# FFN width 2752 as 2560 rows by Strassen and 192 rows without

## The chip, the cores and the metric

The kernel runs on one core of one Trainium2 chip. The metric is the device time of one execution in microseconds; before the change it is 2451.41 us, the median of three runs (2449.39 to 2451.61). Everything is computed in f32.

The names of the engines in the profile: PE is TensorE's matmul, PEld its weight load, DVE is VectorE, ACT is ScalarE, POOL is GpSimd, SP is SyncE, which here issues most of the DMAs.

## What is computed

`x` has 32 samples of 64 positions by 1024 features, in all 2048 tokens. Four residual layers follow each other. The last one is an FFN with low-rank adapters, and it is the one that changes:

```python
x = x + L0(x)                       # a long convolution over the feature axis
x = x + einsum('bsi,boi->bso', x, w1[ids1])     # one 1024x1024 weight for each sample
x = x + einsum('bij,bkj->bik', x, w2[ids2])     # the same again
# L3, with H = 1024, F = 2752, rank 16, one adapter for each sample
gate = x @ W_gate.T + 0.5 * (x @ A_gate.T) @ B_gate.T
up   = x @ W_up.T   + 0.5 * (x @ A_up.T)   @ B_up.T
act  = silu(gate) * up
x = x + act @ W_down.T + 0.5 * (act @ A_down.T) @ B_down.T
```

`A_*` and `B_*` are chosen for each sample by an index that is read on the device.

## The kernel before

Tokens run along the free axis and features along the partitions. The 2048 tokens are four chunks `c` of 512 (8 samples); `x` of a chunk is a tile of 128 partitions x 8 x 512. The program first does the convolution for all chunks, then the two adapter layers for chunk 0 (`adapter`, matmuls at L176, one 512 KB weight `wa` after the other), then `ffn(c)` for each chunk. The adapter layers of chunk c + 1 are cut into 16 pieces that `between` and `other` place among the FFN's matmuls of chunk c, at a rate that spreads them over the chunk: a piece falls due after a share of the hidden products and of the down products. The first piece falls due in the first tile. `x` of chunks 2 and 3 is parked in HBM (`park`) and loaded again (L454) in the first tile of the chunk before, into the buffer of a chunk that has been written out.

The FFN's hidden rows are split in two halves of 1376, each into eleven tiles `m` of up to 128 rows, so that the last tile of each half has 96. A tile `m` takes the same rows from both halves, and its products are done by the Strassen-Winograd scheme with seven instead of eight products of half the size: `stationary` (L337 to L340) forms four sums of weight quarters on VectorE, `moving` (L344 to L347) four sums of the token side, `product` (L367) runs 28 matmuls of 128x128 weights with 256 tokens for `gate` and 28 for `up`, and L381 to L396 gather the seven results from PSUM. In `gated`, before this, `gather` (L214) fetches the tile's rows of `B` from HBM by an indirect DMA on POOL into the one buffer `bgu`, `expand` (L309) runs 16 matmuls of 32 rows for the low-rank part, which lie side by side in the array four at a time, and ACT copies their four banks to `lt` (L319). Then `silu` and the multiplication give `act` (L402 to L404).

The tiles go in two blocks, six and five. After a block the down projection runs over four row blocks `h`, each with seven accumulators in four PSUM banks and one set of matmuls (L507) for each of up to three tiles. The low-rank part of `W_down` is first contracted (`low_rank_down`, L266, into `tm_d`, L278 to L284); in the last block `expand_down` (L292) adds it with matmuls of 64 rows, two side by side. L531 to L542 add the result to `x`, and after the last block L546 writes it out. In the last two row blocks the next chunk's `prepare` runs the contraction with `A_gate` and `A_up` (also L266) and forms the token sums.

The order on PE is the order of the program text; the other engines' orders come from a scheduler. PSUM has eight banks, taken in turn. Weights of all kinds share nine buffers of 512 KB (`wpool`), loaded by SP in order.

The lines that set the width before the change:

```python
F = 2752
FH = F // 2
FM = (FH + P - 1) // P        # 11
BLOCKS = ((0, 6), (6, FM))
SEG = 3
```

Of the kernel before, what the change touches and what calls it, by code (L numbers as in the profile page):

```python
# [24 lines left out]
FH = F // 2  # L25
FM = (FH + P - 1) // P
BLOCKS = ((0, 6), (6, FM))
MB = 6
# [29 lines left out]
CO_BM = CO_OFF + FM  # L58
# [4 lines left out]
def kernel(  # L63
# [18 lines left out]
    bd: bass.AP,  # L82
    out: bass.AP,
# [47 lines left out]
    il = cpool.tile([P, NCK], I32, tag="il", name="il")  # L131
    nc.sync.dma_start(il, ids_lora)
    rowf = cpool.tile([P, NCK], F32, tag="rowf", name="rowf")
# [3 lines left out]
    rows = cpool.tile([P, NCK, FM], I32, tag="rows", name="rows")  # L137
    for c in range(NCK):
        nc.vector.tensor_scalar(
            rows[:, c, :],  # L140
            cst[:, CO_OFF : CO_OFF + FM],
            rowf[:, c : c + 1],
            None,
            ALU.add,
        )
# [66 lines left out]
    def gather(table, c, piece, width, tag, name, bufs):  # L212
        t = gpool.tile([P, width], F32, tag=tag, name=name, bufs=bufs)
        nc.gpsimd.indirect_dma_start(  # L214
            out=t,
            out_offset=None,
            in_=table,
            in_offset=bass.IndirectOffsetOnAxis(
                ap=rows[:, c, piece : piece + 1], axis=0
            ),  # L220
        )
        return t
# [26 lines left out]

    FIRST, SECOND = slice(0, P // 2), slice(P // 2, P)  # L250
    tms = {}
    for name, width in (("g", 2 * H), ("u", 2 * H), ("d", TH)):
        tms[name] = hpool.tile([P, width], F32, tag=f"tm_{name}", name=f"tm_{name}")
    nc.vector.memset(tms["d"], 0.0)
# [4 lines left out]
    def low_rank(at, n, x_of, name):  # L259


        ps = ps_tile(f"pl_{name}")[:, : 2 * H]
        for i in range(n):
            x_i, k = x_of(i)
            for j in range(BC // 2):
                nc.tensor.matmul(  # L266
                    ps[pair(j)],
                    at[:k, i, pair(j)],
                    x_i[:, 2 * H * j : 2 * H * (j + 1)],
                    start=(i == 0),  # L270
                    stop=(i == n - 1),
                )
        return ps

    def low_rank_down(at, n, x_of, name, more):
        ps = low_rank(at, n, x_of, name)
        v = gpool.tile([P, 2 * H], F32, tag="tv", name=f"tv_{name}", bufs=1)
        nc.vector.tensor_mul(v, ps, bmask)  # L278
        for j in range(BC // 2):
            t = tms["d"][pair(j), 2 * H * (j % 2) :][:, : 2 * H]  # L280
            if more:
                nc.vector.tensor_add(t, t, v[pair(j)])
            else:
                nc.vector.tensor_copy(t, v[pair(j)])  # L284

    def expand_down(pairs):
# [3 lines left out]
        for two in pairs:  # L290
            for rows_, (ps, b) in zip((FIRST, SECOND), two):
                nc.tensor.matmul(  # L292
                    ps,
                    b[rows_],
                    tms["d"][rows_],
                    start=False,
# [3 lines left out]

    def expand(bt, n, name):


        banks = [ps_tile(f"pe{j}_{name}") for j in range(BC // 2)]
        for g in range(2):
            for i in range(2):
                for j, ps in enumerate(banks):
                    at_ = (2 * g + i) * 2 * H
                    nc.tensor.matmul(  # L309
                        ps[:n, at_ : at_ + 2 * H],  # L310
                        bt[pair(j), g, i, :n],
                        tms["gu"[g]][pair(j)],
                        start=(g + i == 0),
                        stop=True,
                        skip_group_check=True,
                    )
        lt = gpool.tile([P, 4, TC], F32, tag="lt", name=f"lt_{name}", bufs=1)
        for j, ps in enumerate(banks):
            nc.scalar.copy(  # L319
                lt[:n, :, 2 * H * j : 2 * H * (j + 1)],  # L320
                ps[:n].rearrange("p (i t) -> p i t", i=4),
            )
        return lt.rearrange("p (g i) t -> p g i t", g=2)
# [26 lines left out]
    def gated(c, m, xb, between):  # L350

        n = min(P, FH - m * P)
        bt = gather(bgu, c, m, 4 * P, "bgu", f"bgu_{c}_{m}", 1)
        bt = bt.rearrange("p (g i f) -> p g i f", g=2, i=2)
        lt = expand(bt, n, f"{c}_{m}")
        cs = []
        for g, w in enumerate((wg, wu)):
# [7 lines left out]
            def product(ps, j, start):  # L365
                for kt in range(KH):
                    nc.tensor.matmul(  # L367
                        ps,
                        ws[j][:, kt, :n],
# [7 lines left out]
            pa, pb, pc = (ps_tile(f"pf{i}_{name}")[:n, :TH] for i in range(3))  # L377
# [3 lines left out]
            nc.scalar.copy(u[:n], pa)  # L381
            product(pb, 5, True)
            nc.scalar.copy(cq[:n, 3], pb)  # L383
            nc.vector.tensor_add(u[:n], cq[:n, 3], u[:n])
            product(pc, 6, True)
            nc.vector.tensor_add(cq[:n, 3], pc, u[:n])
            product(pb, 4, True)
            nc.vector.tensor_add(cq[:n, 3], pb, cq[:n, 3])  # L388
            product(pa, 1, False)
            nc.scalar.copy(cq[:n, 0], pa)  # L390
            product(pb, 2, False)
            nc.vector.tensor_add(cq[:n, 1], pb, u[:n])  # L392
            product(pc, 3, False)
            nc.vector.tensor_add(cq[:n, 2], pc, u[:n])
            cf = cq[:n].rearrange("p q t -> p (q t)")
            nc.vector.tensor_add(cf, cf, lt[:n, g].rearrange("p i t -> p (i t)"))  # L396
# [4 lines left out]
        a = act[:n].rearrange("p i (t n) -> p (i t) n", t=2)  # L401
        nc.scalar.activation(a, cs[0][:n], AF.Sigmoid)  # L402
        nc.vector.tensor_mul(a, a, cs[0][:n])
        nc.vector.tensor_mul(a, a, cs[1][:n])  # L404
        return act

    def prepare(c, name):
# [3 lines left out]
        ps = low_rank(at, KT, lambda i: (x_c[:, i, :], P), f"{name}_{c}")  # L411
# [15 lines left out]
    def ffn(c, xb, others):  # L427
# [29 lines left out]

        for block, (m0, m1) in enumerate(BLOCKS):
            nm = m1 - m0
            at = columns(ad[:, block, :, : 2 * nm], c, 2 * nm, f"d{block}_{c}")  # L460
            acts = []
            for m in range(m0, m1):
                acts.append(gated(c, m, xb, between))

            def k_of(m):
                return min(P, FH - m * P)

            def act_of(i):
                k = k_of(m0 + i % nm)
                return acts[i % nm][:k, i // nm], k  # L470

            last = m1 == FM
            if last:
                bt = gather(bd, c, 0, L, "bd", f"bd_{c}", 1)
                bt = bt.rearrange("p (i h f) -> p i h f", i=2, f=P)
                nc.vector.tensor_sub(bt[SECOND, 0], bt[SECOND, 0], bt[SECOND, 1])

            ab = []
            for i, act in enumerate(acts):
                k = k_of(m0 + i)  # L480
                t3 = apools[0].tile([P, 4, TH], F32, tag="actd", name=f"actd_{c}_{m0 + i}")
                q = [act[:k, h, t * TH : (t + 1) * TH] for h in (0, 1) for t in (0, 1)]
                ab.append(moving(*q, *(t3[:k, j] for j in range(4))))

            for h in range(KH):
# [9 lines left out]
                for s0 in range(m0, m1, SEG):  # L495
                    nt = min(SEG, m1 - s0)
                    wt = []
                    for i in (0, 1):
                        t = wpool.tile([P, 2, KH, P], F32, tag="w", name=f"wd{i}_{name}_{s0}")
                        nc.sync.dma_start(t[:, :, :nt], wd[i, h, :, :, s0 : s0 + nt])  # L500
                        wt.append(t)
                    ws = stationary(wt, nt, f"{name}_{s0}")
                    for j in (0, 5, 6, 4, 1, 3, 2):
                        for i in range(nt):
                            m = s0 + i
                            k = k_of(m)
                            nc.tensor.matmul(  # L507
                                pss[j],
                                ws[j][:k, i, :],
# [5 lines left out]
                        if j == 4 and last and s0 + nt == m1:  # L515
                            b = bt[:, :, h]
                            expand_down(
                                (
                                    ((pss[1], b[:, 0]), (pss[4], b[:, 1])),
                                    ((pss[3], b[:, 1]), (pss[2], b[:, 0])),  # L520
                                )
                            )
                    if h == 0 and s0 == m0:
                        low_rank_down(at, 2 * nm, act_of, f"d{block}_{c}", block > 0)
# [286 lines left out]
def _constants(np):  # L811
# [11 lines left out]
    c[:, CO_OFF : CO_OFF + FM] = NE * R * np.arange(FM)  # L823
# [4 lines left out]
def _layouts(np, v):  # L828
    cont = np.ascontiguousarray

    def pad(a, axis, size):
        width = [(0, 0)] * a.ndim
        width[axis] = (0, size - a.shape[axis])
        return np.pad(a, width)
# [27 lines left out]
    def halves(w, axis):  # L862
        w = np.moveaxis(w, axis, 0).reshape(2, FH, -1)
        return pad(w, 1, FM * P).reshape(2, FM, P, -1)

    def hidden(w):
        w = halves(w, 0).reshape(2, FM, P, KT, P)
        return w.transpose(0, 1, 4, 3, 2).reshape(2, FM, P, L)


    wd = halves(v["L3_cond_W_down"], 1).reshape(2, FM, P, 2, KH, P)
    wd = wd.transpose(3, 4, 2, 0, 1, 5)
# [7 lines left out]
    a = halves(v["L3_cond_A_down"][0].reshape(NE * R, F), 1)  # L880
    a = a.reshape(2, FM, P, NE, R).transpose(3, 2, 0, 1, 4)
    ad = np.zeros((NE, len(BLOCKS), P, 2 * MB, R), np.float32)
    for i, (m0, m1) in enumerate(BLOCKS):
        ad[:, i, :, : 2 * (m1 - m0)] = a[:, :, :, m0:m1].reshape(NE, P, -1, R)

    def b_rows(b):
        b = halves(b[0].transpose(1, 0, 2).reshape(F, NE * R), 0)
        return b.transpose(1, 3, 0, 2).reshape(FM, NE * R, 2 * P)
# [52 lines left out]
```

## Time and profile before

One execution was profiled; its own time is 2448.96 us and its span, from the first to the last instruction, 2447.3 us.

| quantity | value |
|---|---|
| median of three runs | 2451.41 us |
| profiled execution, its span | 2448.96 us, 2447.3 us |
| mean granted TensorE clock | 0.995 |
| L367, hidden products | 4928 matmul instructions |
| L507, down products | 2464 matmul instructions |
| L176, adapters | 8192 matmul instructions |
| L292, second low-rank product of `W_down` | 128 matmul instructions |
| moved by DMA | 501.24 MB, mean 205 GB/s |

An f32 matmul of the program is two instructions in the profile. Busy times of single matmuls overlap[...]; the time a matmul costs is therefore read from the distance between the starts of successive ones. In the tables of the profile `out<-in` names the tiles, and what follows is partitions x elements; "idle before" is the time in which the engine did nothing just before an instruction, and what ended that. The granted clock is the share of TensorE's full clock that it was allowed.

### The profile page before, as it was taken

To read this page: it belongs to the slowest core of one execution; us is meant where nothing else is said; L and a number is where in the kernel's file an instruction comes from. 1 tells how busy PE (TensorE), PEld (TensorE's weight loads), DVE (VectorE), ACT (ScalarE), POOL (GpSimd) and SP (SyncE) were. 2 spreads that over 40 slices of the span, in tenths; PEclk is the share of its full clock that TensorE was granted. 3 is DMA by queue.
4 is the path that set the end of the run, shared out by engine and by line. 5 is a ranking of instruction groups with operands and counts; after the bars stand their busy time and mean duration, and the time that the engine had idled before them with its cause. 6 is when DMAs were issued, how large, how long until landed. Compare 5 with 4: busy or idle time off the path is not lost.

```text
span 2447.3 us, 47048 instructions
## 1 busy us (share of the span) xinstructions
PE 2353.5 (96%) x19488; PEld 1877.8 (77%) x19488; DVE 1166.1 (48%) x2264; ACT 313.2 (13%) x613; POOL 204.0 (8%) x286
## 2 busy tenths in 40 slices
PE   3898888999999999999999999999999999999999
PEld 3896336888877787877877787878877788888887
DVE  8811114544345544544344544544354545654554
ACT  3200002111011101110011101110011102110110
POOL 3533001000000020000000020000000020000000
PEclk9999999999999999999999999999999999999999
DMA  6789998565567547565566547565566543323221
GB/s 238 253 292 366 408 408 336 190 236 168 190 224 254 181 146 266 209 217 182 175 244 231 179 152 258 207 216 190 177 244 218 184 149 113 89 76 111 87 65 61
DMA packets 162967, 501.24 MB, mean 205 GB/s; under 512 B 19842, under 2 KB 53954, under 8 KB 161730
## 3 DMA queue, kind: packets, MB, share of 16 engines
q1 hardware_dynamic: 146338, 461.76, 54.2%
q0 software_dynamic: 9504, 27.80, 3.4%
q10 hardware_dynamic: 6912, 8.69, 1.0%
q8 instruction: 153, 2.51, 0.4%
q14 instruction: 60, 0.49, 0.1%
HBM read 485.29 MB, written 12.88 MB: 204 GB/s over the span
## 4 chain that ended last, share of the span: by engine, by line
PE 87%; issue 6%; DMA 3%; DVE 2%; POOL 0%; POOLq 0%; SPq 0%; ACT 0%; DVEq 0%; ACTq 0%
PE pf L367 43%; PE po L507 22%; PE pa L176 14%; PE pc L782 5%; PE pe L309 2%; PE pl_d L266 1%; PE po L292 1%; DMA x<-xd 1%; DMA early<-in_w 0%; DMA wf<-in_wu 0%; POOL x L798 0%; DMA out_y<-x 0%; DMA hk<-kp 0%; DMA raw_g<-in_ag 0%; DMA ln<-in_lens 0%
## 5 line engine op out<-in xcount | busy, mean ns | idle before, releaser
L367 PE MATMUL pf<-xd,wf 128*128 128x256 f32 (+1 forms) x2816 | 667.3, 381 | 0.0
L367 PEld LDWEIGHTS pf<-xd,wf 128*128 128x128 f32 (+1 forms) x2816 | 523.0, 187 | 89.1 <-issue 7.5
L176 PE MATMUL pa<-wa,x 128*32 128x256 f32 x8048 | 472.5, 384 | 33.9 <-DMA wa<-in_w 26.7
L367 PE MATMUL pf<-xd,s 128*128 128x256 f32 (+1 forms) x2112 | 499.2, 379 | 2.9 <-ACT c L383 1.7
L367 PEld LDWEIGHTS pf<-xd,s 128*128 128x128 f32 (+1 forms) x2112 | 395.8, 188 | 63.6 <-ACT c L383 2.1
L176 PEld LDWEIGHTS pa<-wa,x 128*32 128x32 f32 x8048 | 249.5, 111 | 249.8 <-DMA wa<-in_w 67.4
L507 PE MATMUL po<-act,wd 128*128 128x256 f32 x704 | 177.0, 385 | 0.0
L507 PE MATMUL po<-actd,s 128*128 128x256 f32 x704 | 172.9, 379 | 0.0
L507 PE MATMUL po<-actd,wd 128*128 128x256 f32 x704 | 172.9, 379 | 0.0
L782 PE MATMUL pc<-uf,hk 128*128 128x256 f32 (+7 forms) x1024 | 153.4, 313 | 17.0 <-DMA hk<-kp 16.7
L214 POOL DMA_INDIRECT bgu<-in_bgu,rows x44 | 45.9, 1044 | 1431.7 <-PE pe L309 1428.2
L782 PEld LDWEIGHTS pc<-uf,hk 128*128 128x128 f32 x1024 | 148.8, 196 | 21.3 <-DMA hk<-kp 9.6
L392 DVE TENSOR_TENSOR c<-pf,u 128x256 f32<-128x256 f32 (+1 forms) x88 | 37.4, 425 | 266.3 <-PE pf L367 266.3
L507 PEld LDWEIGHTS po<-act,wd 128*128 128x128 f32 x704 | 130.6, 190 | 28.0 <-issue 10.2
L507 PEld LDWEIGHTS po<-actd,s 128*128 128x128 f32 x704 | 133.6, 190 | 18.4
L507 PEld LDWEIGHTS po<-actd,wd 128*128 128x128 f32 x704 | 133.6, 190 | 18.4
L319 ACT COPY lt<-pe 128x512 f32<-128x512 f32 (+1 forms) x176 | 90.3, 598 | 372.8 <-PE pe L309 268.9
L337 DVE TENSOR_TENSOR s<-wf 128x512 f32<-128x512 f32 x88 | 59.9, 681 | 119.7 <-DMA wf<-in_wu 44.9
L396 DVE TENSOR_TENSOR c<-c,lt 128x1024 f32<-128x1024 f32 (+1 forms) x88 | 107.7, 1224 | 6.7
L187 DVE STREAM_TRANSPOSE y<-pa 128x512 f32<-128x512 f32 x64 | 45.5, 711 | 137.1 <-PE pa L176 137.1
L337 DVE TENSOR_TENSOR s<-wd 128x384 f32<-128x384 f32 x64 | 33.4, 521 | 137.5 <-PE po L507 97.4
L388 DVE TENSOR_TENSOR c<-pf,c 128x256 f32<-128x256 f32 (+1 forms) x88 | 37.3, 424 | 105.4 <-PE pf L367 105.2
(150 smaller groups left out, 1713.6 us busy)
## 6 DMA issues: line engine op xcount, KB each, us to landing
wa<-in_w SPq DMA_DIRECT2D x503, 512.0 KB, 7.6
wf<-in_wg SPq DMA_DIRECT2D x88, 512.0 KB, 4.4
wf<-in_wu SPq DMA_DIRECT2D x88, 512.0 KB, 5.2
wd<-in_wd SPq DMA_DIRECT2D x96, 384.0 KB, 4.5
hk<-kp SPq DMA_DIRECT2D x32, 1024.0 KB, 7.9
x<-in_xt SPq DMA_DIRECT2D x4, 2048.0 KB, 10.6
uf<-in_xf SPq DMA_DIRECT2D x16, 512.0 KB, 6.1
wd<-in_wd SPq DMA_DIRECT2D x32, 256.0 KB, 3.4
```

The costliest lines, as they stand in the source:

```text
L176: nc.tensor.matmul(acc[i * S : (i + 1) * S, s * 256 : (s + 1) * 256], xs[c][:, kt, lo + s * S : lo + (s + 1) * S], wt[:, i * 256 : (i + 1) ...
L187: nc.vector.transpose(y, acc)
L214: nc.gpsimd.indirect_dma_start(out=t, out_offset=None, in_=table, in_offset=bass.IndirectOffsetOnAxis(ap=rows[:, c, piece : piece + 1], axis=0
L309: nc.tensor.matmul(ps[:n, at_ : at_ + 2 * H], bt[pair(j), g, i, :n], tms["gu"[g]][pair(j)], start=(g + i == 0), stop=True, skip_group_chec ...
L319: nc.scalar.copy(lt[:n, :, 2 * H * j : 2 * H * (j + 1)], ps[:n].rearrange("p (i t) -> p i t", i=4),)
L337: nc.vector.tensor_add(s1, a21, a22)
L367: nc.tensor.matmul(ps, ws[j][:, kt, :n], xb[j][:, kt, :], start=start and kt == 0, stop=kt == KH - 1, skip_group_check=True,)
L388: nc.vector.tensor_add(cq[:n, 3], pb, cq[:n, 3])
L392: nc.vector.tensor_add(cq[:n, 1], pb, u[:n])
L396: nc.vector.tensor_add(cf, cf, lt[:n, g].rearrange("p i t -> p (i t)"))
L507: nc.tensor.matmul(pss[j], ws[j][:k, i, :], ab[m - m0][j], start=(m == m0 and home[j] % 2 == 0), stop=(m == m1 - 1), skip_group_check=True,)
L782: nc.tensor.matmul(ps[:, j, d * B :], hk[:, j, d * P : (d + 1) * P], uf[:, i + j, : KT - d, :].rearrange("p k b -> p (k b)"), start=(d == ...
```

## The change

The hidden rows are no longer padded. 2560 of them are 2 x 10 full tiles and keep the Strassen scheme, in two blocks of five tiles. The other 192 are computed without it, once per chunk, at the start of `ffn` by a new function `rest`:

- 128 rows of `gate` and 128 of `up`, each as eight matmuls with all 512 tokens, and a third such set whose 128 rows are the last 64 of `up` and the last 64 of `gate`. That is 24 matmuls of 128x128 by 512. Their low-rank parts come from one more expansion with three results instead of four.
- `rest1` holds the activations of the 128 rows, `rest2` those of the last 64 in partitions 64 to 127. The intermediate values use a buffer of the tag of the Strassen sums, `s`.

In the down projection four more matmuls ("tails") for each row block and block of tiles add these rows to four of the seven accumulators. In the first block they carry the 128 rows; their weights come with the last load of the block, which is as wide as before since the block has a tile less. In the last block their contraction has the last 64 rows of `W_down` in partitions 64 to 127 and the low-rank rows of `B_down` in partitions 0 to 63, where `rest2` has received the contracted low-rank values. `expand_down` goes. The tile `wl` for this is filled by two indirect gathers on POOL and two loads on SP for each chunk.

```diff
-FH = F // 2
-FM = (FH + P - 1) // P
-BLOCKS = ((0, 6), (6, FM))
-MB = 6
+FM = F // (2 * P)
+FH = FM * P
+REST = P // 2
+BLOCKS = ((0, FM // 2), (FM // 2, FM))
+MB = FM // 2
...
+    def rest(c):
+        bt = b_rows(c, FM)
+        for i in range(3):
+            wt = wpool.tile([P, KT, P], F32, tag="w", name=f"wr{i}_{c}")
+            nc.sync.dma_start(wt.rearrange("p k f -> p (k f)"), wr[i])
+            if i == 2:
+                lt = expand(bt, f"{c}_rest", (("g", 0), ("u", 1), ("u", 2), ("g", 2)))
+                nc.vector.tensor_add(cs[0], pss[0], lt[:, 0])
+                nc.vector.tensor_add(cs[1], pss[1], lt[:, 1])
+                nc.scalar.activation(rest1, cs[0], AF.Sigmoid)
+                nc.vector.tensor_mul(rest1, rest1, cs[0])
+                nc.vector.tensor_mul(rest1, rest1, cs[1])
+            elif i == 0:
+                pss = []
+                cr = gpool.tile([P, 3, KH, P], F32, tag="s", name=f"cr_{c}")
+                cs = [cr[:, j].rearrange("p k f -> p (k f)") for j in range(3)]
+            ps = ps_tile(f"pr{i}_{c}")
+            for kt in range(KT):
+                nc.tensor.matmul(
+                    ps,
+                    wt[:, kt, :],
+                    xs[c][:, kt, :],
+                    start=(kt == 0),
+                    stop=(kt == KT - 1),
+                )
+            pss.append(ps)
+        v, up = cs[2], cs[0]
+        nc.vector.tensor_add(v, pss[2], lt[:, 2])
+        nc.scalar.copy(up[SECOND], v[FIRST])
+        a = rest2.rearrange("p i t -> p (i t)")
+        nc.gpsimd.memset(a[FIRST], 0.0)
+        nc.scalar.activation(a[SECOND], v[SECOND], AF.Sigmoid)
+        nc.vector.tensor_mul(a[SECOND], a[SECOND], v[SECOND])
+        nc.vector.tensor_mul(a[SECOND], a[SECOND], up[SECOND])
...
-                bt = gather(bd, c, 0, L, "bd", f"bd_{c}", 1)
-                bt = bt.rearrange("p (i h f) -> p i h f", i=2, f=P)
-                nc.vector.tensor_sub(bt[SECOND, 0], bt[SECOND, 0], bt[SECOND, 1])
+                wl = gpool.tile([P, 2, 2, L // 2], F32, tag="wl", name=f"wl_{c}", bufs=1)
+                for t in (0, 1):
+                    wl_t = wl[:, t].rearrange("p i f -> p (i f)")
+                    gather(wl_t[FIRST], bd, rows_half[FIRST, c, t : t + 1])
+                    nc.sync.dma_start(wl_t[SECOND], wd_rest)
+                nc.vector.tensor_sub(wl[:, 1, 0], wl[:, 1, 0], wl[:, 1, 1])
...
                     for j in (0, 5, 6, 4, 1, 3, 2):
+                        if end and j in tails:
+                            w, t = tails[j]
+                            a = rest2[:, t] if last else rest1[:, t * TH : (t + 1) * TH]
+                            nc.tensor.matmul(
+                                pss[j], w, a, start=False, stop=False, skip_group_check=True
+                            )
...
-                        if j == 4 and last and s0 + nt == m1:
-                            b = bt[:, :, h]
-                            expand_down(
-                                (
-                                    ((pss[1], b[:, 0]), (pss[4], b[:, 1])),
-                                    ((pss[3], b[:, 1]), (pss[2], b[:, 0])),
-                                )
-                            )
```

The host's layouts follow: the weights of the 192 rows are their own arrays (`wr`, `wd_rest`), and the tables of `A_down`, `B_gate` and `B_up` have one more piece.

## The prediction

> **What bounds the kernel now.** First the busy shares and the chain of waits on the page, then the longest waits of TensorE after 420 us, the busy time by chunk, and last the chain in order of time inside a chunk and at its edges.
>
> ```profile
> PE 2353.5 (96%) x19488; PEld 1877.8 (77%) x19488; DVE 1166.1 (48%) x2264; ACT 313.2 (13%) x613; POOL 204.0 (8%) x286
> ...
> PE 87%; issue 6%; DMA 3%; DVE 2%; POOL 0%; POOLq 0%; SPq 0%; ACT 0%; DVEq 0%; ACTq 0%
> ...
> PE pa L176 <- DMA x<-xd: 5.9, 2, 3.3
> ...
> 377.00:924.60 547.60, 543.92 (x4634) 432.79 (x4626) 263.14 (x488) 70.64 (x138) 39.18 (x62) 1.00 0.61 210
> 924.60:1470.40 545.80, 543.21 (x4589) 433.40 (x4589) 262.54 (x490) 67.99 (x136) 29.61 (x44) 1.00 0.60 207
> 1470.40:2019.00 548.60, 545.29 (x4589) 433.57 (x4588) 261.94 (x488) 67.99 (x136) 30.65 (x44) 0.99 0.60 205
> 2019.00:2441.90 422.90, 422.90 (x2406) 364.35 (x2406) 227.82 (x443) 60.07 (x130) 9.70 (x10) 1.00 0.29 86
> ```
>
> (A page line counts busy time, the next the chain's shares; the third says that TensorE's only waits of over 0.1 us after 420 us are two for x.) The last four rows are the four FFN chunks (stretch, its length, PE, PEld, DVE, ACT, POOL busy, granted clock, DMA share). TensorE fills them but for 3.7, 2.6, 3.3 and 0.0 us; VectorE is at half. A busy PE need not be at its peak, so I read the spacing of its matmuls. In the chain each row is start, length, what; the last two are from TensorE's timeline:
>
> ```profile
> 639.18 36.46 PE po L507 x168
> ...
> 2019.03 1.10 PE pe L309 x32
> 2020.13 24.37 PE pf L367 x112
> 2044.50 1.10 PE pe L309 x32
> ...
> 2390.77 15.33 PE po L507 x70
> 2406.10 1.06 PE po L292 x8
> ...
> 2035.71 1.89 PE L367 MATMUL pf<-xd,wf 128*128 128x256 f32 x8
> 2037.43 1.89 PE L367 MATMUL pf<-xd,s 128*128 128x256 f32 x8
> ```
>
> One hidden tile costs 25.47 us (2019.03 to 2044.50), and eight 128x256 instructions start 1.727 us apart (2035.71 to 2037.43 is 1.72, ten such steps 17.27): 0.216 us each, for every operand and place. An f32 matmul is two of them, 0.432 us. The FFN is limited by how many columns pass the array, so the change is a count of matmuls first, and then a question of what happens at the four chunk starts.
>
> **Matmuls, per chunk.** *Gone:* the eleventh hidden tile, 25.47 us; it has only 96 rows but costs what a full one does (24.34 against 24.37 us for its 112). *Added:* `rest`, 3 x 8 matmuls of 128x512 and 16 small expansion products. No row has 512 columns. The nearest are two of 256: 24 x 2 x 0.432 = 20.7 us. Could a wide one save a fixed share? The convolution's L782 grows from 278 to 361 ns between 128 and 224 columns, 0.86 ns a column; a whole one has 216/256 = 0.84, so no fixed share is left, and the lower end is 20.7 less some tenths. The upper end the trace leaves open (rival c). I take 20.7, plus 1.10 for its expansion (that of L309) and 0.1 at the switches: 21.9. Net -3.6.
>
> *Down projection:* before, a row block h takes 18.23 us in the first block (two of them are 36.46 us for 168) and 15.33 + 1.06 = 16.39 in the second, so 4 x 34.62 = 138.5. After, each h of either block has 35 Strassen products and 4 tails, 78 instructions: 18.23 x 78/84 = 16.93, times 8 = 135.4. Net -3.1. Here a rule speaks against the change. The Trainium skill, TensorEngine Tiling (Array Packing), Performance Considerations, says that a contraction of 64 or less should be packed by row tiling for up to 2x; the change replaces just such packed products (L292) by full ones. By the rule four packed products would cost 2 x 0.432 = 0.86 us; the row says 1.06. With the rule's price the net would be -2.3 a chunk instead of -3.1; I use the row. And the full products aren't a loss against packing, since their other 64 rows carry W_down.
>
> Low-rank products L266: 22 x 4 before and after. The adapters' pieces are spread over 105 shares a chunk instead of 113, which shifts them by a product or two; none stalled before. Bytes are level: 4 x 512 KB of the tile go, 3 x 512 and 2 x 256 come, and the tails' W_down columns ride in loads of three tiles as large as those before. Sum: 4 x (-3.6 - 3.1) = **-26.8 us**.
>
> **Chunk starts, what goes.** At chunks 1 and 2 the first adapter stalls on the next chunk's x:
>
> ```profile
> 926.50 6.79 DMA out_y<-x
> 933.51 7.78 DMA x<-xd
> 941.42 7.11 PE L176 MATMUL pa<-wa,x 128*32 128x256 f32 x128 [2.59 <-DMA x<-xd]
> 1487.16 9.94 PE L176 MATMUL pa<-wa,x 128*32 128x256 f32 x128 [3.31 <-DMA x<-xd]
> 1485.00:1490.00 5.00, 2.84 (x28) 1.57 (x32) 1.86 (x2) 1.06 (x1) 0.00 (x0) 0.61 0.70 287
> ```
>
> The load waits for the old x to be written out, and lands 17 us after the last down product (924.6 to 941.4). After the change 21.9 us of `rest` stand before the first tile, so that adapter comes 35 us after. In SP's order it stood behind the adapter's seventh weight and stands behind the fourth now; new ahead of it are only the two loads of 64 rows of W_down, which wait for the gathers of `wl`, so it may go out some 2 us later than before. Both stalls go, -5.9; with the second goes the clock drop (0.61): 9.94 against 7.1 us, -2.9. In chunk 0 the stalls 0.70 (L309 on tm_u), 1.69 (L367 on ACT, which copies at_d first) and 1.25 (L367 on VectorE, whose weights came late) stand just where `rest` now goes, -3.6. Sum **-12.4**.
>
> **Chunk starts, what comes.** The gather of B rows has one buffer. Before, each had a whole tile (25 us or more). The first tile's gather must now wait for the expansion in `rest`, with only its third product, 6.9 us, as cover:
>
> ```profile
> 926.93 0.98 POOL L214 DMA_INDIRECT bgu<-in_bgu,rows  x1 [3.01 <-PE pe L309]
> DMA to landing us min/median/max: 6.9/6.9/6.9
> DMA to landing us min/median/max: 7.6/7.6/7.6
> DMA to landing us min/median/max: 14.0/14.0/14.0
> ```
>
> These are landings of gathers at the starts of chunks 1 and 2, and of that of chunk 0's second tile, issued behind 4 MB of parked x; chunk 3's was 6.8. The Trainium skill, DMA: Bandwidth & Descriptors, Anatomy of one DMA, gives 2.0 us plus bytes over 436 GB/s, for 256 KB an estimate of 2.6 us: then there's no stall. By the rows it starts 0.45 us after the expansion (926.48 to 926.93) and lands late: 0.45 + 6.9, 7.6, 6.8 - 6.9 gives 0.4, 1.1 and 0.3 us; in chunk 0, between 7 and 14 us, 0.5 to 7.5: I take 2, since the gather comes 9 us later than that one and most of the parked data has passed. Sum **+3.8**. On POOL's queue the memset of `rest2` and the two gathers of `wl` now stand ahead of it; they wait for the last chunk's tails only, so are issued by 4 us into `rest`, 11 us before.
>
> Other waits at nothing: on VectorE the subtraction on `wl` stands before the first two additions of `rest`. It waits for gather and two loads, about 13 us into `rest` (gather issue 2, landing 7, load 4); the additions are due at 17, PE needs them at 22. If that cover failed, bank and stationaries for the first tile would come late one for one. After `rest`, ACT's copy and sigmoid of 64 rows (about 0.6 us each, by the 599 ns of L319) stand before the copies of the first tile's expansion: 5.2 us against the 6.3 until PE wants a bank back. The tail of the last block at h = 0 waits for a multiplication, an addition and four small copies: 0.29 + 0.29 + 4 x 0.22 = 1.5 us beside six products, 2.6 us. VectorE itself loses work.
>
> **Sum:** 2448.96 (the profiled execution, span 2447.3) - 26.8 - 12.4 + 3.8 = 2413.6. The median of the runs shown is 2451.41, 2.45 more; part of that may be the same clock drop. I say **2414 us**.
>
> **Rivals.**
> (a) *The counted gain alone* (20%): the starts give nothing, because new waits take the place of the removed ones: gather at 10 to 11 us, 4 us late in four chunks, is +16 instead of +3.8: 2426. For it: x load and gather now overlap. Against: DMA engines are at 0.6 there.
> (b) *No change* (3%): the gather as in the 14.0 us row at every chunk, 0.45 + 14 - 6.9 = 7.6 us, and 2.9 for the clock as at 1487: 42 us in four, 2448.96 - 39.2 + 42 = 2452. Against: only the 4 MB ahead in its own queue made 14.0, and that happens once.
> (c) *Slower* (4%): a wide matmul takes the columns beyond 256, the second half of a bank, at half the rate: 0.65 us an instruction instead of 0.43, 10.4 us a chunk in `rest`, 41 in all: 2455. It decides from 35.4 / 82.8 = 43% above two narrow ones, 0.62 us. For: no row has this width. Against: nothing in the rows grows faster than its columns.
> (d) *The change does not do what it says*: excluded by the order of instructions, where 2240 hidden-tile products stand for 2464, 96 wide ones are new, and the down projection has 1248 for 1296.
>
> Likeliest, 73%: 2414, its own range 2408 to 2420. The range for 8 in 10 reaches into (a): **2406 to 2427**. A measurement tells 0.2%, 5 us, from no change: faster 0.93, same 0.03, slower 0.04.
>
> **What would show it.** Chunk 3, without adapters: 422.9 before, 416 to 417 after. `pr` instructions 0.43 us apart. No idle of L176 on x. An idle of L309 on the gather of 0 to 2 us at each chunk start, more in chunk 0. Wrong if that idle is above 5, if VectorE stands waiting for `wl` when the expansion of `rest` ends, or if a wide matmul is off 0.43.

## The result and the profile after

The changed kernel takes 2414.20 us (median of four runs, 2413.37 to 2416.34) where the kernel before, run beside it, takes 2451.51 (2449.39 to 2452.13). The ratio is 0.9857, with a 95% interval of 0.9845 to 0.9869: 1.4% faster. The same kernel run again beside the kernel before, on another chip (*a2* below), took 2416.33, 0.9867 (0.9851 to 0.9884), so the gain is known to a few us and no closer: 37.3 in the first pair of medians, 32.4 in the second, 35.1 between the two profiled executions. The profiled execution took 2413.82 us, its span is 2412.2.

The first rows are the page's busy line and the shares of the chain of waits; then TensorE's waits after 370 us (what, us in total, times, longest); then the four chunks, each from its first product of `rest` to the next chunk's.

```profile
PE 2322.5 (96%) x19136; PEld 1834.6 (76%) x19136; DVE 1115.7 (46%) x2192; ACT 306.7 (13%) x597; POOL 209.9 (9%) x294
...
PE 88%; DMA 9%; DVE 2%; SPq 0%; issue 0%; ACT 0%; POOL 0%; DVEq 0%; ACTq 0%
```

```profile
PE pe L303 <- DMA bgu<-in_bgu,rows: 2.1, 1, 2.1
...
PE pa L182 <- DMA wa<-in_w: 0.8, 4, 0.2
PE pf L359 <- ACT c L375: 0.4, 1, 0.4
```

```profile
381.50:920.20 538.70, 536.14 (x4497) 422.30 (x4498) 249.03 (x469) 69.02 (x134) 38.20 (x59) 1.00 0.62 213
920.20:1455.80 535.60, 535.60 (x4497) 422.15 (x4497) 249.17 (x470) 66.37 (x132) 31.21 (x46) 1.00 0.60 210
1455.80:1991.50 535.70, 535.70 (x4498) 422.26 (x4497) 249.26 (x470) 66.37 (x132) 31.37 (x46) 1.00 0.61 210
1991.50:2407.20 415.70, 415.70 (x2316) 353.93 (x2316) 217.23 (x429) 58.55 (x126) 11.57 (x12) 1.00 0.29 87
```

TensorE's wait on x, the largest of before, is gone from the list. In chunks 1 to 3 TensorE is busy for the whole stretch; in chunk 0 it lacks 2.6 us, the first and the third of these waits (the second lies before it). The kernel is as much bound by TensorE as before, with 352 matmul instructions less.

The chain of waits in order of time, at the start of chunk 3 and in two down-projection row blocks, shows what the count was made of:

```profile
1991.47 13.73 PE pr L419 x32
2005.21 1.10 PE pe_rest L303 x32
2006.31 7.06 PE pr L419 x16
2013.37 1.10 PE pe L303 x32
...
2373.74 12.52 PE po L556 x58
...
2390.57 12.52 PE po L556 x58
```

`rest` takes 13.73 + 1.10 + 7.06 = 21.9 us, and a wide instruction 13.73 / 32 = 0.429 us. A row block of the down projection takes 2390.57 - 2373.74 = 16.83 us.

Placed side by side, with each chunk taken from its first instruction on TensorE to the next chunk's, and chunk 3 to the end of its last down products. The rows show such an edge before and after, and then the last four products of each:

```profile
924.42 1.03 PE L507 MATMUL po<-act,s 128*128 128x256 f32 x4
925.37 0.73 PE L309 MATMUL pe<-tm_g,bgu 32*128 32x128 f32 x16
...
919.17 1.03 PE L556 MATMUL po<-act,s 128*128 128x256 f32 x4
920.03 12.18 PE L419 MATMUL pr<-x,wr 128*128 128x512 f32 x28
...
2441.71 1.03 PE L507 MATMUL po<-act,s 128*128 128x256 f32 x4
...
2407.24 1.03 PE L556 MATMUL po<-act,s 128*128 128x256 f32 x4
```

| stretch | before, us | after, us | difference | predicted |
|---|---|---|---|---|
| to the start of chunk 0 | 378.4 | 381.4 | +3.0 | 0 |
| chunk 0 | 547.0 | 538.6 | -8.4 | -8.3 |
| chunk 1 | 545.0 | 535.6 | -9.4 | -8.9 |
| chunk 2 | 548.6 | 535.6 | -12.9 | -11.8 |
| chunk 3 | 423.6 | 416.8 | -6.8 | -6.4 |
| the end | 4.7 | 4.1 | -0.7 | 0 |
| sum | | | -35.1 | -35.4 |

(The prediction's rows of before put the edge of chunks 0 and 1 at 924.6, where VectorE goes on with `x`; four down products run after that, and the next chunk's first instruction starts at 925.37.) The four chunks gained 2.1 us more than the prediction's steps gave them, the end 0.7, and the stretch before them took 3.0 more. The total hides all three, so the experiments had to look at the parts.

### The profile page after: what moved, and what is told of

Read it like the earlier page. It is cut to its first block, busy times and chain, and to the rows that moved or that the text cites. A ratio compares the mean times of both kernels' runs of the same rounds, so it can differ in the third digit from the quotient of the medians.

```text
span 2412.2 us, 46245 instructions
## 1 busy us (share of the span) xinstructions
PE 2322.5 (96%) x19136; PEld 1834.6 (76%) x19136; DVE 1115.7 (46%) x2192; ACT 306.7 (13%) x597; POOL 209.9 (9%) x294
## 4 chain that ended last, share of the span: by engine, by line
PE 88%; DMA 9%; DVE 2%; SPq 0%; issue 0%; ACT 0%; POOL 0%; DVEq 0%; ACTq 0%
PE pf L359 40%; PE po L556 20%; PE pa L182 14%; DMA wa<-in_w 7%; PE pc L823 5%; PE pr L419 3%; PE po L551 2%; PE pe L303 2%; PE pl_d L275 1%; DMA hk<-kp 1%; DMA wl<-in_wd_rest 1%; DMA early<-in_w 0%; PE pl_u L275 0%; PE pl_g L275 0%; DMA ln<-in_lens 0%
## 5 line engine op out<-in xcount | busy, mean ns | idle before, releaser
L359 PE MATMUL pf<-xd,wf 128*128 128x256 f32 x2560 | 607.2, 381 | 0.0
L359 PEld LDWEIGHTS pf<-xd,wf 128*128 128x128 f32 x2560 | 481.6, 190 | 75.4 <-issue 7.4
L359 PE MATMUL pf<-xd,s 128*128 128x256 f32 x1920 | 453.6, 379 | 0.4 <-ACT c L375 0.4
L359 PEld LDWEIGHTS pf<-xd,s 128*128 128x128 f32 x1920 | 364.7, 190 | 50.4 <-ACT c L375 0.8
L556 PE MATMUL po<-act,wd 128*128 128x256 f32 x640 | 161.7, 383 | 0.0
L556 PE MATMUL po<-actd,wd 128*128 128x256 f32 x640 | 159.0, 379 | 0.0
L384 DVE TENSOR_TENSOR c<-pf,u 128x256 f32<-128x256 f32 x80 | 33.9, 424 | 242.3 <-PE pf L359 242.3
L313 ACT COPY lt<-pe 128x512 f32<-128x512 f32 x160 | 82.1, 600 | 307.5 <-PE pe L303 216.1
L388 DVE TENSOR_TENSOR c<-c,lt 128x1024 f32<-128x1024 f32 x80 | 97.9, 1224 | 6.7 <-DVE c L386 0.5
L419 PE MATMUL pr<-x,wr 128*128 128x512 f32 x192 | 84.2, 595 | 0.0
```

The lines of the kernel that those rows point to most:

```text
L313: nc.scalar.copy(lt[:, :n, 2 * H * j : 2 * H * (j + 1)], ps[:, : n * 2 * H].rearrange("p (i t) -> p i t", i=n),)
L359: nc.tensor.matmul(ps, ws[j][:, kt, :], xb[j][:, kt, :], start=start and kt == 0, stop=kt == KH - 1, skip_group_check=True,)
L388: nc.vector.tensor_add(cf, cf, lt[:, g].rearrange("p i t -> p (i t)"))
L419: nc.tensor.matmul(ps, wt[:, kt, :], xs[c][:, kt, :], start=(kt == 0), stop=(kt == KT - 1),)
L556: nc.tensor.matmul(pss[j], ws[j][:, i, :], ab[m - m0][j], start=(m == m0 and home[j] % 2 == 0), stop=(m == m1 - 1), skip_group_check=True,)
```

## The experiments

Twelve more runs follow, in four groups, each on one chip with the kernel before beside it (medians 2448.91, 2448.70, 2448.20, and one run of 2447.84). Three of them repeat a kernel: the changed one (a2), the one before (b2), and e8. Small differences are read inside a group, or from the traces.

**e1: `rest` in the middle of the chunk.** The theory said that `rest` at the chunk's start is worth more than its count, because it stands between the end of one chunk and the first adapter.

```diff
-        rest(c)
         tv = None
...
+            if not last:
+                rest(c)
             ins = [act[:, i, :] for i in (0, 1) for act in acts]
```

> The changed kernel with the call of rest moved from the start of each chunk to behind the first block's last hidden tile, with the same instructions. Theory (part of the gain, about 12 us, comes from where rest stands: it fills the waits of the chunk starts): chunks 1 and 2 stall on x again by 2.6 and 3.3 us, with up to 2.9 us more where the clock drops, chunk 0 loses about 3.6 us again, and the 2.1 us wait for the first tile's gather goes because a whole tile covers the gather; 2414.2 + 7 to 10 gives 2421 to 2424 us. Rival (only the count of matmuls matters, the waits would have gone or stayed anyway): 2412 to 2416 us.

Measured: 2436.41 us (2435.39 to 2439.20). The loss was 12 to 15 us larger than expected. TensorE's waits in this kernel (line numbers in the variants are shifted by a few, and L359 is now the hidden product), and one of them from the timeline (here VectorE's and TensorE's rows; in brackets the idle time before, and what ended it):

```profile
PE pf L359 <- DVE c L380: 8.5, 3, 3.5
PE pf L359 <- ACT c L375: 7.3, 1, 7.3
PE pa L182 <- DMA x<-xd: 1.6, 1, 1.6
```

```profile
937.36 0.69 DVE L506 TENSOR_TENSOR wl<-wl 128x512 f32<-128x512 f32 x1 [10.33 <-DMA wl<-in_bd,rows_half]
...
939.50 3.78 PE L359 MATMUL pf<-xd,s 128*128 128x256 f32 x8 [3.03 <-DVE c L380]
```

The change's own new wait appears here: VectorE stands 10.33 us before the subtraction on `wl`, the additions that free TensorE's banks are queued behind it, and TensorE idles 3.03 us; the next eight instructions then take 3.78 us instead of 1.89. In the changed kernel VectorE waits just as long (9.10 us before the subtraction at 929.79) and nobody notices, because `rest` has its 21.9 us to run. So the placement of `rest` covers that wait too, as the prediction had it ("late one for one" if the cover failed). The size of the x part was left open by this run.

**e2: the kernel before, with its first adapter piece one product later.** This takes the x stall of before away without anything of the change.

```diff
-            other(AT_GATED)
+            if i or c == 0:
+                other(AT_GATED)
```

> The kernel before, with the first adapter piece of chunks 1 to 3 due one product later (12 us), and nothing else changed. Theory (x is there 17 us after the last down product, and only the first piece was too early for it): both waits for x go, 5.9 us, and the clock drop with the second, up to 2.9: 2451.5 - 6 to 9 gives 2442 to 2446 us. Rival (the wait moves to the next thing, such as the adapter's last weight or the piece that is now left for the end of the chunk): 2449 to 2453 us.

Measured: 2440.51 us (2438.05 to 2442.13), 8.4 us below the kernel before in the same group; ratio 0.9968 (0.9955 to 0.9980). No wait on x is left, and in its trace chunks 1 and 2 take 542.7 and 542.5 us, 2.3 and 6.1 less than before. The prediction had put 5.9 for the stalls and 2.9 for the half clock after one of them, 8.8 in all: confirmed.

**e3: two buffers for the gathered rows**, in the changed kernel.

```diff
-... tag="bgu", name=f"bgu_{c}_{piece}", bufs=1)
+... tag="bgu", name=f"bgu_{c}_{piece}", bufs=2)
```

> The changed kernel with two buffers for the gathered B rows instead of one, so that the first tile's gather goes out before the expansion in rest. Theory (the 2.1 us idle of TensorE in chunk 0 is the gather's): that idle goes or shrinks to the next late thing there, the additions behind the subtraction on wl, which would leave about 1 us; chunks 1 to 3 don't change; 2412 to 2413.5 us. Rival (the W_down rows wl, which VectorE awaits in chunk 0 until 402.4 us, are the real limit): the idle stays at about 2 us, 2414 us.

Measured: 2416.11 us (2415.68 to 2418.57). That is 0.9868 (0.9851 to 0.9884) of the kernel before beside it, so nothing is won that these runs could tell. The idle on the gather is gone, but TensorE's list shows another wait, and VectorE's timeline at the start of chunk 0 says why.

```profile
PE pf L359 <- ACT c L375: 3.2, 1, 3.2
```

```profile
405.50 0.69 DVE L505 TENSOR_TENSOR wl<-wl 128x512 f32<-128x512 f32 x1 [21.93 <-DMA wl<-in_wd_rest]
406.11 0.68 DVE L408 TENSOR_TENSOR cr<-pr,lt_rest 128x512 f32<-128x512 f32 x1
...
406.83 0.63 ACT L410 ACTIVATE rest<-cr 128x512 f32<-128x512 f32 x1 [5.64 <-DVE cr L408]
```

In chunk 0 the second load of `wl` goes out at 390.7 us, just after the two transfers of 2 MB that park x (389.0 and 389.9), and takes 14.7 us. VectorE waits 21.93 us for them, `rest`'s additions come late, ACT's sigmoid (in order) waits for those, and ACT's copy out of PSUM for the first tile stands behind the sigmoid. The gather had only been the later of two waits.

**e5: the low-rank products apart again.** The changed kernel, but with the four packed products of 64 rows (`expand_down`) back in the last block; the tails keep all 128 rows, with zeros where the low-rank values were.

```diff
-                t = rest2[pair(j % 2), j // 2, 2 * H * (j % 2) :][:, : 2 * H]
+                t = tms["d"][pair(j), 2 * H * (j % 2) :][:, : 2 * H]
...
+                        if j == 4 and last and end:
+                            b = bt[:, :, h]
+                            expand_down(
+                                (
+                                    ((pss[1], b[:, 0]), (pss[4], b[:, 1])),
+                                    ((pss[3], b[:, 1]), (pss[2], b[:, 0])),
+                                )
+                            )
```

> The changed kernel without its second part: the low-rank products of W_down are done by 64-row matmuls of their own again, as before the change, and the last 64 rows of W_down keep full matmuls whose other 64 rows multiply zeros. Theory (a packed set of four costs 1.06 us a row block, and sharing the array saves all of it): 16 row blocks x 1.06 = 17 us more, 2431 us, and 16.84 us a row block of the last tiles becomes 17.9. Rival by the rule of two-fold packing: 16 x 0.86 = 13.8, 2428 us. Second rival (the packed ones hide beside the full ones): 2414 to 2418 us.

Measured: 2436.97 us (2435.57 to 2440.84). The chain inside a row block:

```profile
862.15 0.43 PE po L569 x2
862.58 0.86 PE po L574 x4
863.45 1.06 PE po L300 x8
864.51 0.63 PE po L569 x2
865.14 0.86 PE po L574 x4
```

The packed set takes 1.06 us, and the tail after it 0.63 instead of 0.43: it costs 1.26 us, 16 times 1.26 = 20.2 us. Chunks 1 to 3 of the trace are 5.05 us longer each than in the changed kernel, which is four such sets. So the shared tails are more than half of what the change gained: without tails that carry the low-rank rows and rows of `W_down` in one contraction, the kernel is only 11.9 us faster than the one before it in the same group. The rule of full packing, 0.86 us a set, would make 13.8.

**a2, e6, e8, e4, on one chip.** *a2* is the changed kernel again; *e6* is e1 with the subtraction on `wl` held back on VectorE; *e8* is e3 with the same; *e4* has each wide matmul of `rest` as two narrow ones. The edit that holds the subtraction back:

```diff
+            add = nc.vector.tensor_add(cf, cf, lt[:, g].rearrange("p i t -> p (i t)"))
+            if (m, g) == (1, 0):
+                marks.append(add.ins)
...
+                with tc.issue_after(marks[-1]):
+                    nc.vector.tensor_sub(wl[:, 1, 0], wl[:, 1, 0], wl[:, 1, 1])
```

> The changed kernel as it is, run beside the next three for differences of 1 or 2 us: 2413 to 2416. The second low-rank product of chunk 0 ended at 381.5 us in its first profile and at 378.4 in that of the kernel before. If the change itself makes the stretch before 380 us longer, it ends at 381 or later again; if it is chance from run to run, nearer to 379.

Measured: 2416.33 us (2413.94 to 2417.22), 0.9867 (0.9851 to 0.9884) of the kernel before; `pl_u` ended at 379.7.

> Rest in the middle as in e1, but the subtraction on wl is held back on VectorE until the second tile's first addition. Theory: of the 22 us that e1 lost, what stood behind that subtraction (8.5 us of TensorE's waits in chunks 1 to 3, and about 2 us of half clock after each) comes back, and what stays is the copy of at_d in chunk 0 (7.3) and the wait on x (1.6): 2421 to 2425. Rival, the loss came from rest's other cover (gathers, x, ACT): 2432 or more.

Measured: 2433.85 us (2432.74 to 2435.66), so the rival's number. The wait behind `wl` is gone as meant, but TensorE's waits are these:

```profile
PE pa L182 <- DMA x<-xd: 9.4, 2, 5.2
PE pf L361 <- ACT c L377: 5.3, 1, 5.3
```

```profile
943.33 9.67 PE L182 MATMUL pa<-wa,x 128*32 128x256 f32 x128 [4.20 <-DMA x<-xd]
...
1486.77 9.31 PE L182 MATMUL pa<-wa,x 128*32 128x256 f32 x128 [5.17 <-DMA x<-xd]
```

The stall behind VectorE in e1 had merely delayed TensorE until x was there. With it away the x stall of before is back, larger (4.20 and 5.17 us where it was 2.59 and 3.31), and so is the half clock, after both now (9.67 and 9.31 us for an adapter's products instead of 7.11). My expectation was wrong, and what it had left out is what the prediction had said first: at a chunk's start x is 17 us away, and `rest` is what stands in that time.

> The changed kernel with two buffers for the gathered rows and the subtraction on wl held back until the second tile's first addition. Theory: in chunk 0 the gather (2.1 us) and behind it wl (3.2 us in e3) were the last two waits of TensorE; with both gone no wait above 0.5 us is left after 390 us, 2 us less than the changed kernel beside it: 2411 to 2413. Rival, a third wait stands right behind them (weights of the first tile, landing while x is parked): no gain, 2414.

Measured: 2412.42 us (2409.46 to 2414.08), 3.9 less than the changed kernel beside it; the runs of the two just touch (2413.94 is that one's lowest), so the trace has to speak. In it no wait above 0.3 us is left after 380 us, and chunk 0 takes 535.7 us, as long as chunks 1 and 2 (535.6), where it took 538.6 and 540.5 (a2) in the changed kernel. The theory holds: gather and `wl` were the last two waits of chunk 0, and no third stood behind them.

> Each 128x512 matmul of rest as two of 128x256. By columns alone 24 x 2 x 2 x 0.216 = 20.7 us a chunk against 20.6 measured (48 x 0.429): 0 to 0.2 us a chunk, so within 1 us of the changed kernel. Rival, that wide ones save a fixed share (or cost one): apart by more than 2 us in all.

```diff
-                nc.tensor.matmul(
-                    ps,
-                    wt[:, kt, :],
-                    xs[c][:, kt, :],
...
+                for t in (0, 1):
+                    nc.tensor.matmul(
+                        ps[:, t * TH : (t + 1) * TH],
+                        wt[:, kt, :],
+                        xs[c][:, kt, t * TH : (t + 1) * TH],
```

Measured: 2415.42 us (2413.10 to 2418.50). Its chain at the start of chunk 3, to be laid beside that of the changed kernel above:

```profile
1992.48 13.81 PE pr L420 x64
2006.30 1.10 PE pe_rest L303 x32
2007.40 7.10 PE pr L420 x32
```

13.81 against 13.73, 7.10 against 7.06: 0.12 us a chunk. Columns cost the same in either width.

**b2, e9, e8 again: the 3 us before chunk 0.** Up to there nothing runs that the change edits on TensorE. But until chunk 0 starts, TensorE waits for adapter weights alone, and the change issues its first two gathers of `wl` among them. In windows of 2 us of the changed kernel's trace (the last number is GB/s, the one before the DMA engines' busy share) the rate falls in the last few us before each gather has landed (issued at 220.7 and 233.4, landing some 8 us later):

```profile
224.00:226.00 2.00, 1.34 (x28) 0.50 (x16) 1.41 (x2) 0.00 (x0) 1.93 (x4) 1.00 1.08 358
226.00:228.00 2.00, 0.18 (x4) 0.00 (x0) 0.00 (x0) 0.00 (x0) 0.79 (x2) 1.00 1.01 260
...
236.00:238.00 2.00, 1.26 (x24) 0.57 (x24) 0.00 (x0) 0.00 (x0) 0.00 (x0) 1.00 1.06 412
238.00:240.00 2.00, 0.92 (x16) 0.26 (x9) 0.98 (x2) 0.00 (x0) 0.00 (x0) 1.00 1.04 258
```

> The kernel before, once more, for the stretch up to the second low-rank product of chunk 0, which ended at 378.4 us (before) and 377.9 (e2, the same up to there), but at 379.8 to 383.2 in the seven profiles of the changed kernel and its variants. If that is the change, 377.5 to 379 again; if it is chance, up to 381.

Measured: `pl_u` ended at 377.0, the total was 2448.05 us.

e9 is e8 with the gathers and loads of `wl` for chunk 0 issued later:

```diff
+                    with ExitStack() as after:
+                        if c == 0:
+                            after.enter_context(tc.issue_after(cols[-1]))
+                        gather(wl_t[FIRST], bd, rows_half[FIRST, c, t : t + 1])
+                    with ExitStack() as after:
+                        if c == 0:
+                            after.enter_context(tc.issue_after(wfs[-1]))
+                        nc.sync.dma_start(wl_t[SECOND], wd_rest)
```

> As e8, but in chunk 0 the two gathers and two loads of wl go out after the second block's columns and the last tile's weights, not amid the adapters' weights. Theory: each of the two gathers of 64 partitions costs the loads around it (the 2 us slices at 226 and 238 us fell to about 260 GB/s from 400, 0.7 us each), so TensorE, which waits for those loads alone, is 1.5 to 2 us earlier at the second low-rank product: its end 378 to 379 instead of 380 to 381, no such dip, total 1 to 2 us under e8. Rival: the loads are late for another reason: no difference before 380 us.

> e8 beside e9 on the same chip: 2410 to 2413; the second low-rank product of chunk 0 ends at 380 to 381, with the dip in the loads at both gathers of wl.

Measured: e9 2408.65 us (2406.24 to 2410.16), e8 2410.84 (2409.17 to 2412.35). The total and the rate came as expected, the end of `pl_u` did not: 380.7 for e9, 381.6 for e8. The DMA's bytes in two windows tell why; the column of SP's queue, which loads the weights, leaves the gathers out:

| kernel | moved by 210 us, MB | 210 to 245 us, GB/s | of it SP's queue, MB | `pl_u` ends, us |
|---|---|---|---|---|
| before, e2, b2 | 56.59, 56.84, 57.15 | 396, 396, 396 | 11.96, 11.95, 11.94 | 378.4, 377.9, 377.0 |
| after, a2, e8, e8 again | 56.36, 56.92, 56.66, 56.55 | 373, 371, 373, 373 | 11.14, 11.09, 10.89, 10.88 | 381.5, 379.7, 380.0, 381.6 |
| e9, without those gathers | 55.68 | 394 | 12.17 | 380.7 |
| e10 (below), gathers of 128 partitions | 56.49 | 395 | 11.39 | 379.3 |

With the gathers the rate is down by 23 GB/s for 35 us, 0.8 MB, which is 2 us at the 408 GB/s of the stretch behind. e9 has the full rate, but it had moved 0.9 MB less than e8 by 210 us, most of it in the convolution. There the runs scatter: by 0.6 MB in three runs of the code of before, by 1.2 MB in those of the changed one. So 2 of the 3 us belong to the gathers; the other one is no larger than that scatter, and whether the change has a part in it stays open. The kernel before has a gather there too, of `bd`: one of 512 KB over 128 partitions, as many bytes as the two of 256 KB over 64, and its weights came at the full rate.

**e10: is it the gathers, or their shape?** The changed kernel with the two gathers over 128 partitions instead of 64, twice the bytes, the upper half overwritten by the loads that follow.

```diff
-                    gather(wl_t[FIRST], bd, rows_half[FIRST, c, t : t + 1])
+                    gather(wl_t, bd, rows_half[:, c, t : t + 1])
```

> The changed kernel with the two gathers of wl over all 128 partitions (512 KB each; the upper half is overwritten by the loads of W_down's rows as before). Between 210 and 245 us the DMA moved 396 GB/s in three profiles of the kernel before (one gather of 128 partitions, 512 KB), 371 to 375 in nine with the two gathers of 64 partitions, 394 in e9 without them. If it is the gathers' shape (64 partitions keep only part of the DMA engines at work, and the loads around them wait for the rest), the rate goes back to 390 to 396, with 0.5 MB more to move. If it is that there are two more gathers of whatever shape, it stays at 375 or falls.

Measured, for the window from 210 to 245 us of e10 and then of the changed kernel, and last SP's queue in the same window of e10, the changed kernel and the kernel before (packets, MB, share of the DMA engines' time):

```profile
210.00:245.00 35.00, 27.34 (x452) 13.42 (x446) 4.23 (x6) 1.04 (x1) 13.40 (x22) 1.00 1.03 395
```

```profile
210.00:245.00 35.00, 26.70 (x428) 12.55 (x420) 4.23 (x6) 1.04 (x1) 13.69 (x22) 0.95 1.03 373
```

```profile
q1 hardware_dynamic: 3129, 11.39, 84.2%
...
q1 hardware_dynamic: 3058, 11.14, 86.3%
...
q1 hardware_dynamic: 3288, 11.96, 88.0%
```

The fall of the rate belongs to the shape: twice the bytes, and the full rate. But the rate is not what TensorE waits for. Half of the gathers' bytes are thrown away here, and the weights gained 0.25 MB of the 0.82 that they had lost, some 0.6 us; `pl_u`'s end, 379.3, is within the scatter of the changed kernel (379.7 and 381.5) or just below it. Its one run took 2414.46 us (before beside it 2447.84). One gather of 128 full partitions, as the kernel before has it, was not tried.

**A version that probably beats both** came out of this: e9, with two buffers for the gathered rows, the subtraction held back, and chunk 0's `wl` late. It takes 0.9834 (0.9820 to 0.9849) of the kernel before beside it. It was not run beside the changed kernel itself: e8 is 3.9 us below that on one chip, and e9 2.2 below e8 on another, where the runs of the two overlap.

## Why the prediction was right, and where it was not

The predicted 2414 us and the measured 2414.20 lie so close by luck: two misses of 2 to 3 us cancel, and the same kernel took 2416.33 in another group. That the time lies in the predicted range is no luck, since the mechanism was the right one. By its steps:

- **The bound.** That TensorE's columns bound the FFN held: chunk 3, which has no adapters and no stalls, was to lose 6.4 us and lost 6.8 (423.6 to 416.8, from its first instruction to the end of its last product). Summed there over the distances from one start on TensorE to the next, the hidden tiles fell from 280.0 to 254.6, `rest` came with 22.0, and the down projection fell from 138.6 to 135.2.
- **`rest` against the eleventh tile, -3.6 a chunk.** Right: 21.9 us predicted, 21.9 to 22.0 measured, and 25.4 gone, -3.4. Rival (c), wide columns at half rate, would have shown 0.65 us an instruction; it is 0.429, and e4 shows that narrow ones cost the same.
- **The down projection, -3.1 a chunk.** It gained 3.4. The working scaled a whole row block, 18.23 us for 84 instructions, to 78; that row stands beside a piece of an adapter and holds some 0.1 us that is not its matmuls' (one after is 16.83 for 78). The rule that speaks for packing (the Trainium skill, TensorEngine Tiling (Array Packing), Performance Considerations) was rightly set below the row: e5 puts the packed set at 1.26 us, even above the row's 1.06. The 0.20 above it agrees with what the same page says under Key Properties, that a change of tiling mode drains the array; the page has no time for it.
- **What goes at the chunk starts, -12.4.** It went. A chunk with adapters and without a stall takes 542.5 to 542.7 us before (e2, chunks 1 and 2) and 535.6 after, so the count is 6.9 to 7.1 there. Chunk 1 was 2.4 above that before, by its stall of 2.59; chunk 2 was 6.0 above it, by 3.31 and the half clock, and gained the most, as it should. The x part, 8.8, was measured alone at 8.4 (e2) and seen to come back when `rest` is moved away (e6). Chunk 0 was 4.4 above it, where the three small stalls had been put at 3.6, and is 3.0 above it after: the gather's 2.1, 0.4 for a wait of L359 on ACT, and half a microsecond beside them. In part the half clock is chance: the second profile of the kernel before (b2) has it after both stalls (3.26 and 3.22 us).
- **What comes, +3.8 for the gather.** In chunk 0 it was 2.1 for the predicted 2. What the prediction left out is the half clock that can follow: it did in the profiles of a2, e4, e5 and e10, which have the same wait (1.89 to 3.06 us), at about 1.5 us. In chunks 1 to 3 it was nothing for the predicted 0.4, 1.1 and 0.3: at chunk 1 it landed in 5.6 us, not in the 6.9 to 7.6 of the rows of before. Neither the rows nor the rule's estimate of 2.6 us was the landing time here; the estimate was the worse, and the conclusion drawn from it the better.
- **Waits at nothing.** Right in the kernel as changed, but thinner than told in one place: in chunk 0 the wait on `wl` was priced as at the other chunks, an end 13 us into `rest`; there it ended 21 us into it. It was hidden behind `rest` and the gather, and it decides as soon as the gather is mended (e3). One of the prediction's own signs of being wrong came up with it: when the expansion of `rest` ended in chunk 0 (396.4 us), VectorE did stand waiting for `wl`, until 402.43. TensorE waited for the gather until 405.69 all the same, so here the sign cost at most the 0.4 on ACT.
- **Missed altogether:** the two gathers of `wl` that go out before chunk 0, 2 us. The prediction followed POOL's queue at the chunk starts, and counted the bytes as level; it did not ask what a gather does to the loads beside it in the stretch before chunk 0, where TensorE waits for loads alone.

Rival (a) needed the gather to be 4 us late in every chunk and (b) 7.6; both fell with that.

## What to carry to other kernels

A block of work without fresh inputs, put where one stage hands over to the next, is worth its cover as well as its count; and taking one of several stacked waits away shows the next one, so mend them together (e3 alone gained nothing that could be told, with the held subtraction chunk 0 had no wait left). Spare rows of a matmul's contraction cost nothing here (a tail takes the 0.43 us of its two instructions whether 64 rows of it are zeros or work), so small products were better put there than packed beside each other. In a stretch that the DMA bounds, look at the shape of every transfer added to it, not at its bytes alone, and count the bytes that are waited for, not the rate.

## What the hardware showed beyond that

- Two gathers over 64 partitions, 256 KB each, took the DMA from 396 to 373 GB/s for 35 us; over 128 partitions, 512 KB each, they left it at 395. That part of the engines stood idle, as the expectation of e10 had it, is not what the rows show: in the slow windows all engines were counted busy (1.01 and 1.04 at 260 and 258 GB/s). With the engines as busy, 152 packets passed in the 2 us from 238 and 228 in the 2 us from 241, so the packets took longer; why they did stays open.
- After 370 us, half clock followed idles of TensorE of 1.89 (e10), 1.98 (e1 and e2), 2.24 (e5) and 2.69 us (e4), and every one of 3.03 (e1) and more; after 1.86 (b2), 2.13 (after) and 2.59 us (before) the clock stayed full. So between 1.9 and 2.7 us both happen, and the length of the idle alone does not decide. Here are the wait and the first eight hidden products after it in e10, the same in the changed kernel, and the granted clock (before the DMA's share) in e10's next 3.3 us:

```profile
403.24 0.73 PE L303 MATMUL pe<-tm_g,bgu 32*128 32x128 f32 x16 [1.89 <-DMA bgu<-in_bgu,rows]
404.55 3.43 PE L359 MATMUL pf<-xd,wf 128*128 128x256 f32 x8
...
405.69 0.73 PE L303 MATMUL pe<-tm_g,bgu 32*128 32x128 f32 x16 [2.13 <-DMA bgu<-in_bgu,rows]
406.79 1.99 PE L359 MATMUL pf<-xd,wf 128*128 128x256 f32 x8
...
404.10:407.40 3.30, 3.30 (x19) 2.54 (x14) 3.30 (x6) 0.00 (x0) 0.86 (x2) 0.50 0.41 136
```

The Trainium skill, TensorE: Matmul & The Clock Gate, Why this matters for your kernels, says to avoid idle of more than about 3 us; here 1.89 us was enough once, so the measurement decides. A wait of 2 us on the gather can cost 2 us or 3.5, and the first profile of the changed kernel shows the cheap case.
